# Another order for TensorE's steps around the two fills in the state-space layer of a two-layer kernel

## The chip, the cores and the metric

The kernel runs on one core of a Trainium2 chip. A core has five engines that run side by side, each through its own instructions in order: TensorE (PE, matrix products; PEld is its loading of weights), VectorE (DVE), ScalarE (ACT), GpSimd (POOL) and SyncE (SP, which issues DMA transfers here). They wait for each other by semaphores. The metric is the device time of one execution in microseconds (us). Everything is float32.

## The reference

The input x is 32 images of 96 channels by 56 x 56 places, L = 3136 places each. Layer 0 is an inverted-bottleneck convolution block (1x1 to 576 channels, 3x3 per channel, squeeze and excitation, 1x1 back, residual). Layer 1 treats the places as a sequence and applies two Mamba blocks, then a fusion with a pooled branch, a batch norm and a residual. The change lies in the Mamba blocks:

```
h   = layernorm(seq)                          # over the 96 channels
xs, z = split(h @ in_w)                       # 192 channels each
xc  = silu(causal_conv_4_taps(xs) + conv_b)
dt, Bm, Cm = split(xc @ xproj_w)              # 6, 16, 16 columns
delta = softplus(dt @ dt_w + dt_b)            # 192 channels
state[d, s] = exp(delta[d] * A[d, s]) * state[d, s] + delta[d] * xc[d] * Bm[s]   # along the places
y   = sum_s state[d, s] * Cm[s] + Dp * xc
seq = seq + (y * silu(z)) @ out_w
```

## The kernel before

Layer 0 takes the first sixth of the time and is the same in both kernels. Layer 1 cuts each image into NQ = 4 chunks of LC = 784 places, so there are 128 chunks, and each passes through two Mamba blocks: 256 **units** of work, `(chunk, block)` in the list `units`. From the fourth chunk on the blocks alternate, block 0 of chunk c and then block 1 of chunk c - 3, so units of the two kinds take turns.

The 192 channels times 16 states of a unit are scanned in NT = 24 **steps** of 128 partitions by 784 places. `place(t)` splits a step into k (0 to 2, a third of the channels), j (0 to 3, a group of four states) and p (0 or 1). One loop counter `at` runs through all 256 x 24 = 6144 steps, and each turn of the loop writes the instructions of one step to every engine:

- `decay` (ScalarE, L934): the factor exp(delta A), into a bank pair of PSUM (tag `da`, two buffers), one step ahead of its scan. For the steps with j = 0 it goes into SBUF instead, three or four steps ahead.
- `inject` (GpSimd, L971): u times B, where u = delta xc ("delta x"), for two steps at once, four steps ahead, for j = 1 to 3.
- `fill` (TensorE, L948): the same product for j = PEJ = 0, the first two steps of every eight. 64 small matmul instructions with a block-diagonal matrix of B (`diag`) and the transposed u (`ut`) write it into a `da` buffer, `bp`. So steps 0 and 1, 8 and 9, 16 and 17 of a unit read a fill, which is written by TensorE in the step before. `fill(at + 1)` needs the buffer that the scan of step at - 1 has read.
- `scan` (VectorE, L982), then `product` with C (VectorE, L990, first 400 places) and `rest` (GpSimd, L998, the other places).
- `reduce` (TensorE, L1019 for Dp xc and L1024 for the sum over states), four steps behind, at every odd step, and `gated` (VectorE, L1035) after each third of the channels.

Everything else of a unit is put among these steps by hand: `prepare(n)` and `finish(n)` return lists of `(t, step)`, where t counts steps from 48 before unit n's first scan (prepare) or from 24 after it (finish). The whole part of t picks the turn of the loop, the fraction sorts within it, and these steps come after `reduce` in that turn. Since everything repeats every 24 steps, one may think of t modulo 24: during the scans of one unit the kernel also projects and stores the unit before it, and prepares the two after it. `bursts` are ScalarE's runs of Silu and Softplus, each with two loads of a function table, before the scan of their turn.

The small steps on TensorE take their output banks from one pool of two (`pp`, by `bank(...)`): layer-norm statistics (`center`, `variance`, `turn`, `turn_back`: tiles cen, var, ct, xn), `conv` (xs), `gate` (z), `project_bc` (bc), `turn_b` (bt), `project_dt` (dt), `turn_u` (ut) and the output projection `project` in `finish` (o). Each bank is free again when ScalarE has copied it out (`square`, `normalise`, `normal`, `keep`, `store_bc`, `diagonal`, `keep_u`, `store`). TensorE works in order, so a step that waits for a bank holds all that is queued behind it, fills and reduces too.

`store` is two plain copies in a unit of block 0, and in a unit of block 1 it is two pairs of activations with accumulated sums, for the batch norm. `root` and `newton` are the inverse square root of the layer norm, on ScalarE and then VectorE. `input_u` makes u in thirds: before, two thirds on VectorE, which reads xc from a bank that ScalarE copies it to (`bring_x`, L802 and L810), and one third on GpSimd (L808). `spread` writes u to DRAM, from where it comes back (`ub`) in the layout of the scan.

Of the kernel before, what the change touches and what calls it, by code (L numbers as in the profile page):

```python
# [26 lines left out]
HB = LC // 2  # L27
# [6 lines left out]
NB = DIN // 64  # L34
# [25 lines left out]
def conv_mamba_kernel(ctx, tc, a, out):  # L60
# [43 lines left out]
    with ExitStack() as ph:  # L104
# [49 lines left out]
        xs, maps, h2s, pools, se = {}, {}, {}, {}, {}  # L154
# [303 lines left out]
    with ExitStack() as ph:  # L458
# [14 lines left out]
        def bank(name):  # L473
            return pp.tile([128, 512], F32, name=name, tag="p")
# [145 lines left out]
        def prepare(n):  # L620
# [14 lines left out]
            def center(h):  # L635
                ps = d["cen", h] = bank(f"cen_{n}_{h}")
                pe.matmul(ps[:C, :HB], cen, seqs[c, i][:, cols(h)], start=True, stop=True)

            def square(h):
                if h == 0:  # L640
                    d["sq"] = wt([128, LC], "sx", 1, n)[:C]
                s.activation(d["sq"][:, cols(h)], d["cen", h][:C, :HB], AF.Square)
# [17 lines left out]
            def newton(step):  # L660
                va, rs = d["va"], d["rs"]
                if step == 0:
                    d["nw"] = wt([TK, NK], "nw", 1, n)
                    v.scalar_tensor_tensor(d["nw"], rs, -0.5, va, ALU.mult, ALU.mult)
                if step == 1:
                    v.tensor_mul(d["nw"], d["nw"], rs)
                if step == 2:
                    to = wt([TK, NK], "rs", 1, n)
                    v.scalar_tensor_tensor(to, d["nw"], 1.5, rs, ALU.add, ALU.mult)
                    d["rs"] = to  # L670
                    if q == 0:
                        g.memset(xn[:, : KC - 1], 0.0)


            def turn(m):
                ps = d["ct", m] = bank(f"ct_{n}_{m}")
                for k in TURNS[m]:
                    o = (k - TURNS[m][0]) * C
                    pe.matmul(ps[:TK, o : o + C], seqs[c, i][:, k * TK : (k + 1) * TK], cen, start=True, stop=True)

            def normalise(m):
                if m == 0:
                    d["xt"] = wt([128, LC], "sx", 1, f"{n}_t")[:TK, : NK * C].rearrange("p (k c) -> p k c", k=NK)
                for k in TURNS[m]:
                    o = (k - TURNS[m][0]) * C
                    s.activation(d["xt"][:, k, :], d["ct", m][:TK, o : o + C], AF.Copy, scale=d["rs"][:, k : k + 1])

            def turn_back(h):
                ps = d["xn", h] = bank(f"xn_{n}_{h}")
                for k in range(NK):  # L690
                    lo, hi = max(k * TK, h * HB), min((k + 1) * TK, h * HB + HB)
                    if lo < hi:
                        pe.matmul(
                            ps[:C, lo - h * HB : hi - h * HB], d["xt"][:, k, :],
                            eye[:TK, lo - k * TK : hi - k * TK], start=True, stop=True,
                        )

            def normal(h):
                to = xn[:C, KC - 1 + h * HB : KC - 1 + h * HB + HB]
                s.copy(to, d["xn", h][:C, :HB])  # L700
# [50 lines left out]
            def spread(tag, t, ks):  # L751
                if tag not in d:
                    d[tag] = udram.tile([DIN, LC], F32, name=f"{tag}d_{n}", tag=f"{tag}d")
                for h in range(2):
                    to = d[tag][:, cols(h)].rearrange("(k m) l -> m k l", k=NB)
                    sp.dma_start(to[:, ks], t[h * 64 : h * 64 + 64, ks])
# [39 lines left out]
            def softplus():  # L796
                through([d["dl"]], AF.Softplus)

            def bring_x(k):

                d["up", k] = bank(f"up_{n}_{k}")
                s.copy(d["up", k][:, :HB], d["xc"][:, k])  # L802

            def input_u(k):

                if k == NB - 1:
                    d["us"] = wt([128, NB, HB], "us", 1, n)
                    g.tensor_mul(d["us"][:, k], d["dl"][:, k], d["xc"][:, k])  # L808
                    return
                v.tensor_mul(d["us"][:, k], d["dl"][:, k], d["up", k][:, :HB])  # L810
                spread("u", d["us"], slice(0, 1) if k == 0 else slice(1, NB))


            steps = [(-20, load)]
            for h in range(2):
                steps += [(-10.4 + h, lambda h=h: center(h)), (-9.8 + h, lambda h=h: square(h))]
            steps += [(-6.4, variance), (-5.8, root), *[(t, lambda m=m: newton(m)) for m, t in enumerate((-5.4, -5.3, -4.9))]]
            for m in range(2):
                steps += [(-4.5 + m, lambda m=m: turn(m)), (-3.9 + m, lambda m=m: normalise(m))]
                steps += [(-2.5 + m, lambda m=m: turn_back(m)), (-1.9 + m, lambda m=m: normal(m))]  # L820
            steps += [(-0.7, trail)]
            for k in range(NB):
                for taps, t in ((((0, 1), 1.5), ((2, 3), 2.5)), (((0,), 2.6), ((1,), 3.5), ((2, 3), 4.5)), (((0, 1), 9.5), ((2, 3), 10.5)))[k]:
                    steps += [(t, lambda k=k, taps=taps: conv(k, taps))]
                steps += [((3.1, 5.1, 11.1)[k], lambda k=k: keep("xc", 3, "xs", k))]
                steps += [((11.5, 12.5, 13.5)[k], lambda k=k: gate(k)), ((12.2, 13.1, 14.1)[k], lambda k=k: keep("z", 3, "zp", k))]
            steps += [(17.5, project_bc), (18.1, store_bc), (18.5, turn_b), (19.1, diagonal)]
            for k in range(NB):
                steps += [(19.6 + k, lambda k=k: project_dt(k)), (20.2 + k, lambda k=k: keep("dl", 1, "dtp", k))]
                steps += [((38.6, 46.6, 52.6)[k], lambda k=k: turn_u(k)), ((39.2, 47.2, 53.05)[k], lambda k=k: keep_u(k))]  # L830
            for m in range(6):
                steps += [(26.9 + m, lambda m=m: scatter(*divmod(m, 3)))]
            steps += [(32.1, lambda: spread("delta", d["dl"], slice(0, NB))), (33.0, lambda: input_u(NB - 1))]
            steps += [(33.6, lambda: bring_x(0)), (34.1, lambda: input_u(0))]
            steps += [(35.2, lambda: bring_x(1)), (36.1, lambda: input_u(1))]
            bursts = [(15, lambda: through([d["xc"], d["z"]], AF.Silu)), (31, softplus)]
            return steps, bursts

        def finish(n):

            c, i = units[n]
            b, q = divmod(c, NQ)
            d = data[n]

            def project(k):
                if k is None:
                    old = seqs.pop((c, i))
                    through = eye[:C, :C] if i + 1 < NL else fusw[:, 0, :]
                    for h in range(2):
                        d["o", h] = bank(f"o_{n}_{h}")  # L850
                        pe.matmul(d["o", h][:C, :HB], through, old[:, cols(h)], start=True, stop=False)  # L851
                    return
                for h in range(2):
                    r = slice(h * 64, h * 64 + 64)
                    pe.matmul(d["o", h][:C, :HB], outw[r, i, k, :], d["z"][r, k, :], start=False, stop=k == NB - 1)  # L855

            def store(h):
                if i + 1 < NL:
                    if h == 0:
                        seqs[c, i + 1] = wt([C, LC], f"seq{i + 1}", 4, n)  # L860
                    s.copy(seqs[c, i + 1][:, cols(h)], d["o", h][:C, :HB])
                    return
                if h == 0:
                    d["pre"] = wt([C, LC], "pre", 1, n)
                at = 2 * c + h
                s.activation(
                    d["pre"][:, cols(h)], d["o", h][:C, :HB], AF.Identity, bias=g2[:, b : b + 1],
                    accum_out=stats[:, 0, at : at + 1],
                )
                if at == 0:  # L870
                    s.activation(pivot, stats[:, 0, 0:1], AF.Copy, scale=-1.0 / HB)
                s.activation(d["o", h][:C, :HB], d["pre"][:, cols(h)], AF.Square, bias=pivot, accum_out=stats[:, 1, at : at + 1])  # L872

            def count():
                if i + 1 == NL:
                    sp.dma_start(pred[b][:, q * LC : (q + 1) * LC], d["pre"])
                data[n] = {}

            return [
                (5.5, lambda: [project(k) for k in (None, 0, 1)]), (6.5, lambda: project(2)),  # L880
                (7.1, lambda: store(0)), (8.1, lambda: store(1)), (9, count),
            ]

        LAG = 4
# [287 lines left out]
```

## Time and profile before

| | |
|---|---|
| median of 3 runs | 20446.33 us (20437.07 to 20451.98) |
| the profiled execution | 20447.55 us, span 20445.7 us |
| first scan to last scan, from the trace | 3462.3 to 20148.8 us |
| busy in the span: PE, DVE, ACT, POOL | 85%, 83%, 69%, 69% |
| mean granted clock of TensorE | 0.868 of full speed |
| DMA engines, mean busy share in layer 1 | 0.67 |

A row of the costliest groups reads: line, engine, operation, tile written <- tiles read, shape, count | busy us in all, mean ns of one | idle us of that engine just before them, and what ended most of it. A row of the timeline reads: start us, length us, engine, line, operation, tiles, shape, count, and in brackets the idle time of the engine before it and what ended that. A row of the windows reads: stretch, its length, then for PE, PEld, DVE, ACT and POOL the busy us with the number of instructions, then the granted clock of TensorE, the busy share of the DMA engines and GB/s.

### The profile page before, as it was taken

The numbers are of one execution on the slowest core, as the hardware profiler recorded it, in microseconds if no ns is written. First come the engines' busy times: TensorE is split into PE (matmuls) and PEld (weight loads), VectorE is DVE, ScalarE is ACT, GpSimd is POOL, SyncE is SP. The second block draws the span as 40 slices with busy tenths as digits, with TensorE's granted clock in tenths as the row PEclk, the third lists the DMA queues.
The fourth block names the chain that finished last, engine by engine and source line by source line (L and its number), as shares of the span: only waits on it lengthen the run. The fifth ranks groups of instructions, "written<-read, shape, count | busy, mean of one in ns | idle before, by whom it ended". The sixth has DMA issues, their size and how long they took to land. (4 is left out here: it accounts for less than half of the span.)

```text
span 20445.7 us, 515066 instructions
## 1 busy us (share of the span) xinstructions
PE 17445.1 (85%) x212796; PEld 8792.3 (43%) x212796; DVE 17046.5 (83%) x13151; ACT 14125.3 (69%) x26028; POOL 14171.2 (69%) x5870
## 2 busy tenths in 40 slices
PE   8999998888888888888888888888888888888883
PEld 4444444444444444444444444444444444444441
DVE  8888886888888888888888888888888888888883
ACT  4444444777777777777777777777777777777774
POOL 0000002888888888888888888888888888888884
PEclk9999998888888888888888888888888888888886
DMA  1000002666666666666666666666666666666668
GB/s 31 25 25 25 25 25 69 166 166 167 168 167 164 165 168 167 168 163 167 166 168 168 166 165 164 166 169 167 168 165 167 165 167 166 169 167 166 163 167 214
DMA packets 1607272, 2946.67 MB, mean 144 GB/s; under 512 B 688790, under 2 KB 901998, under 8 KB 1567814
## 3 DMA queue, kind: packets, MB, share of 16 engines
q1 hardware_dynamic: 1596278, 2875.12, 56.0%
q0 software_dynamic: 6656, 38.54, 0.9%
q8 instruction: 1668, 27.33, 0.6%
q14 instruction: 686, 5.62, 0.1%
q10 hardware_dynamic: 1984, 0.07, 0.0%
HBM read 2456.09 MB, written 455.82 MB: 142 GB/s over the span
## 5 line engine op out<-in xcount | busy, mean ns | idle before, releaser
L971 POOL TENSOR_TENSOR bx<-ub,B 128x1568 f32<-128x1568 f32 x2304 | 8152.6, 3538 | 20.0 <-DMA B<-bcd 20.0
L998 POOL TENSOR_TENSOR hc<-hh,C 128x768 f32<-128x768 f32 x3072 | 5612.6, 1827 | 2840.3 <-DVE hh L982 1831.3
L982 DVE TENSOR_TENSOR_SCAN hh<-da,state,bx 128x784 f32<-128x784 f32 x3456 | 6307.4, 1839 | 68.8 <-ACT da L934 67.2
L934 ACT ACTIVATE da<-deltab,acol 128x784 f32<-128x784 f32 x4608 | 4231.7, 918 | 2390.5 <-DVE hh L982 2376.6
L982 DVE TENSOR_TENSOR_SCAN hh<-bx,state,bp 128x784 f32<-128x784 f32 x1152 | 2124.7, 1844 | 1694.4 <-PE bp L948 1099.2
L990 DVE TENSOR_TENSOR hc<-hh,cp 128x800 f32<-128x800 f32 x3072 | 2954.6, 962 | 0.1
L1024 PE MATMUL y<-hc,rel 128*32 128x392 f32 x24576 | 2834.1, 529 | 27.3 <-issue 22.4
L948 PE MATMUL bp<-diag,ut 91*32 91x91 f32 (+1 forms) x98304 | 2574.4, 254 | 46.0 <-issue 31.1
L948 PEld LDWEIGHTS bp<-diag,ut 91*32 91x32 f32 (+1 forms) x98304 | 2333.3, 110 | 599.9 <-issue 507.5
L389 POOL TENSOR_TENSOR x<-x,x 96x784 f32<-96x784 f32 x128 | 274.5, 2144 | 3056.6 <-ACT x L388 3004.0
L712 PE MATMUL xs<-xn,wx 97*64 97x392 f32 x12288 | 2199.1, 499 | 0.9 <-ACT o L872 0.5
L314 DVE SCALAR_TENSOR_TENSOR h<-hpad,hp,h 128x1568 f32<-128x1568 f32 x1024 | 2037.0, 1989 | 34.3
L728 PE MATMUL z<-xn,wz 97*64 97x392 f32 x3072 | 973.1, 725 | 1268.2 <-DVE us L810 486.2
L982 DVE TENSOR_TENSOR_SCAN hh<-da,bx 128x784 f32<-128x784 f32 x1152 | 2032.0, 1778 | 25.5 <-ACT da L934 25.0
L959 ACT COPY cp<-C 128x400 f32<-128x400 f32 x3072 | 1505.7, 490 | 318.2 <-DVE hc L990 318.2
L934 ACT ACTIVATE bx<-deltab,acol 128x784 f32<-128x784 f32 x1536 | 1435.8, 935 | 0.0
L712 PEld LDWEIGHTS xs<-xn,wx 97*64 97x64 f32 x12288 | 814.0, 136 | 1350.5 <-issue 1256.3
L982 DVE TENSOR_TENSOR_SCAN hh<-bx,bp 128x784 f32<-128x784 f32 x384 | 684.6, 1783 | 626.7 <-PE bp L948 454.1
L288 PE MATMUL dw<-hpad,diag 32*32 32x392 f32 x36864 | 1097.3, 515 | 49.2 <-issue 48.5
L1024 PEld LDWEIGHTS y<-hc,rel 128*32 128x32 f32 x24576 | 605.1, 111 | 1064.7 <-issue 1023.3
L728 PEld LDWEIGHTS z<-xn,wz 97*64 97x64 f32 x3072 | 196.5, 176 | 1964.2 <-ACT xc L723 661.9
L749 PE MATMUL dt<-bcs,wd 64*64 64x392 f32 x3072 | 1020.5, 756 | 0.0
(194 smaller groups left out, 23019.2 us busy)
## 6 DMA issues: line engine op xcount, KB each, us to landing
deltab<-deltad SPq DMA_DIRECT2D x3072, 196.0 KB
ub<-ud SPq DMA_DIRECT2D x3072, 196.0 KB
C<-bcd SPq DMA_DIRECT2D x4096, 98.0 KB
diag<-bdiag SPq DMA_DIRECT2D x256, 1473.8 KB
B<-bcd SPq DMA_DIRECT2D x3072, 98.0 KB
deltad<-dl SPq DMA_DIRECT2D x512, 294.0 KB
ud<-us SPq DMA_DIRECT2D x512, 196.0 KB
ud<-us SPq DMA_DIRECT2D x512, 98.0 KB
```

Of the source, the lines that this page charges most:

```text
L288: pe.matmul(ps[r][to : to + 32, :HB], diag[src, n, t, :], hb[src, r0 : r0 + RB, dx : dx + W], start=t == 0, stop=t == 8, skip_group_check= ...
L314: v.scalar_tensor_tensor(acc, src, tap, acc, ALU.mult, ALU.add)
L712: pe.matmul(d["xs", k][h * 64 : h * 64 + 64, :HB], wx[:, i, o, k * 64 : k * 64 + 64], xn[:, o + h * HB : o + h * HB + HB], start=o == 0, s ...
L728: pe.matmul(ps[h * 64 : h * 64 + 64, :HB], wz[:, i, k * 64 : k * 64 + 64], xn[:, KC - 1 + h * HB : KC - 1 + h * HB + HB], start=True, stop ...
L934: s.activation(das[at], d["delta", k][:, p, :], AF.Exp, scale=acol[:, j, i, 2 * k + p : 2 * k + p + 1])
L948: pe.matmul(ps[sg * DB : sg * DB + DB, o : o + z], d["ut", k][:z, b, h, p * DB : p * DB + DB], dg[:z, sg // 2, h, x : x + z, sg % 2], star ...
L959: s.copy(cps[at], data[n]["C", j][:, :LP])
L971: g.tensor_mul(bx, data[n]["u", k], beside(data[n]["B", j]))
L982: v.tensor_tensor_scan(hhs[at - p][:, p, :], das.pop(at), bxs.pop(at), state[i][:, t : t + 1] if c % NQ else 0.0, ALU.mult, ALU.add,)
L990: v.tensor_mul(hcs[at - 1][:, :, :LP], hhs[at - 1][:, :, :LP], beside(cps.pop(at)))
L998: g.tensor_mul(hcs[at - 1][:, :, LP:], hhs[at - 1][:, :, LP:], beside(data[n]["C", j][:, LP:]))
L1024: pe.matmul(yps[k][r0 : r0 + DB, :HB], rel, hc[:, p, h * HB : h * HB + HB], start=False, stop=j == SG - 1, skip_group_check=True,)
```

## The change

The lists of `prepare` and `finish` get other times. By t modulo 24:

- The output projection (`project`) goes from steps 5 and 6 to 9 and 10, its `store` from 7 and 8 to step 11.
- The convolution of the third third of the channels goes from steps 9 and 10 to 4 and 5, right behind the second.
- `center`, `square`, `variance`, `root`, `newton`, `turn`, `normalise`, `turn_back`, `normal` and `trail` all come one to three steps earlier; `variance` from step 17 to 14, `root` and `newton` from 18 to 16.
- The second `gate` comes right behind the first, in step 11, the third in step 12.
- `turn_u` goes from steps 14, 22 and 4 to 13, 14 and 5. Steps 6 and 22 now have no small TensorE step, nor have 7, 8, 15, 16, 23 and 0, the turns in which the fills themselves are written.
- All three thirds of u are made by GpSimd, in steps 9, 10 and 11, each followed by its own two writes to DRAM. `bring_x` and its bank are gone.

```diff
-            def bring_x(k):
-
-                d["up", k] = bank(f"up_{n}_{k}")
-                s.copy(d["up", k][:, :HB], d["xc"][:, k])
-
             def input_u(k):
 
-                if k == NB - 1:
+                if k == 0:
                     d["us"] = wt([128, NB, HB], "us", 1, n)
-                    g.tensor_mul(d["us"][:, k], d["dl"][:, k], d["xc"][:, k])
-                    return
-                v.tensor_mul(d["us"][:, k], d["dl"][:, k], d["up", k][:, :HB])
-                spread("u", d["us"], slice(0, 1) if k == 0 else slice(1, NB))
-
+                g.tensor_mul(d["us"][:, k], d["dl"][:, k], d["xc"][:, k])
+                spread("u", d["us"], slice(k, k + 1))
 
             steps = [(-20, load)]
             for h in range(2):
-                steps += [(-10.4 + h, lambda h=h: center(h)), (-9.8 + h, lambda h=h: square(h))]
-            steps += [(-6.4, variance), (-5.8, root), *[(t, lambda m=m: newton(m)) for m, t in enumerate((-5.4, -5.3, -4.9))]]
+                steps += [((-11.4, -10.5)[h], lambda h=h: center(h)), ((-10.8, -9.9)[h], lambda h=h: square(h))]
+            steps += [(-9.4, variance), (-7.9, root), *[(t, lambda m=m: newton(m)) for m, t in enumerate((-7.5, -7.4, -7.3))]]
             for m in range(2):
-                steps += [(-4.5 + m, lambda m=m: turn(m)), (-3.9 + m, lambda m=m: normalise(m))]
-                steps += [(-2.5 + m, lambda m=m: turn_back(m)), (-1.9 + m, lambda m=m: normal(m))]
-            steps += [(-0.7, trail)]
+                steps += [(-6.5 + m, lambda m=m: turn(m)), (-5.9 + m, lambda m=m: normalise(m))]
+                steps += [(-4.5 + m, lambda m=m: turn_back(m)), (-3.9 + m, lambda m=m: normal(m))]
+            steps += [(-2.7, trail)]
+            taps = (
+                (((0, 1), 1.5), ((2, 3), 2.5)), (((0,), 2.6), ((1, 2), 3.5), ((3,), 4.5)), (((0, 1), 4.6), ((2, 3), 5.5)),
+            )
             for k in range(NB):
-                for taps, t in ((((0, 1), 1.5), ((2, 3), 2.5)), (((0,), 2.6), ((1,), 3.5), ((2, 3), 4.5)), (((0, 1), 9.5), ((2, 3), 10.5)))[k]:
-                    steps += [(t, lambda k=k, taps=taps: conv(k, taps))]
-                steps += [((3.1, 5.1, 11.1)[k], lambda k=k: keep("xc", 3, "xs", k))]
-                steps += [((11.5, 12.5, 13.5)[k], lambda k=k: gate(k)), ((12.2, 13.1, 14.1)[k], lambda k=k: keep("z", 3, "zp", k))]
-            steps += [(17.5, project_bc), (18.1, store_bc), (18.5, turn_b), (19.1, diagonal)]
+                steps += [(t, lambda k=k, o=o: conv(k, o)) for o, t in taps[k]]
+                steps += [((3.1, 5.1, 6.1)[k], lambda k=k: keep("xc", 3, "xs", k))]
+                steps += [((11.5, 11.6, 12.5)[k], lambda k=k: gate(k)), ((12.1, 12.2, 13.1)[k], lambda k=k: keep("z", 3, "zp", k))]
+            steps += [(17.6, project_bc), (18.2, store_bc), (18.6, turn_b), (19.2, diagonal)]
             for k in range(NB):
                 steps += [(19.6 + k, lambda k=k: project_dt(k)), (20.2 + k, lambda k=k: keep("dl", 1, "dtp", k))]
-                steps += [((38.6, 46.6, 52.6)[k], lambda k=k: turn_u(k)), ((39.2, 47.2, 53.05)[k], lambda k=k: keep_u(k))]
+                steps += [((37.6, 38.7, 53.6)[k], lambda k=k: turn_u(k)), ((38.2, 40.2, 54.2)[k], lambda k=k: keep_u(k))]
             ...
-            steps += [(32.1, lambda: spread("delta", d["dl"], slice(0, NB))), (33.0, lambda: input_u(NB - 1))]
-            steps += [(33.6, lambda: bring_x(0)), (34.1, lambda: input_u(0))]
-            steps += [(35.2, lambda: bring_x(1)), (36.1, lambda: input_u(1))]
+            steps += [(32.1, lambda: spread("delta", d["dl"], slice(0, NB)))]
+            steps += [(33.0 + k, lambda k=k: input_u(k)) for k in range(NB)]
...
             return [
-                (5.5, lambda: [project(k) for k in (None, 0, 1)]), (6.5, lambda: project(2)),
-                (7.1, lambda: store(0)), (8.1, lambda: store(1)), (9, count),
+                (9.5, lambda: [project(k) for k in (None, 0, 1)]), (10.5, lambda: project(2)),
+                (11.1, lambda: store(0)), (11.2, lambda: store(1)), (12, count),
             ]
```

## The prediction

> **What bounds the kernel now.** I read the page first: the span by engine, the clock row and the costliest groups.
>
> ```profile
> PE 17445.1 (85%) x212796; PEld 8792.3 (43%) x212796; DVE 17046.5 (83%) x13151; ACT 14125.3 (69%) x26028; POOL 14171.2 (69%) x5870
> PEclk9999998888888888888888888888888888888886
> L982 DVE TENSOR_TENSOR_SCAN hh<-bx,state,bp 128x784 f32<-128x784 f32 x1152 | 2124.7, 1844 | 1694.4 <-PE bp L948 1099.2
> L982 DVE TENSOR_TENSOR_SCAN hh<-bx,bp 128x784 f32<-128x784 f32 x384 | 684.6, 1783 | 626.7 <-PE bp L948 454.1
> ```
>
> No engine is full, but nearly all of VectorE's idle time in layer 1 stands before the scans that read a fill (bp): 1694.4 + 626.7 = 2321 us, 9.07 us in each of the 256 units. With the scans counted off in order, 24 to a unit (means over units 10 to 239), a unit lasts 65.27 us: 55.44 us without VectorE idle, and idle of 3.29 us before scan 8, 2.87 before scan 16, 2.87 before scan 0 and 0.77 around step 18 (newton waiting for root). The second scan of each pair waits for almost nothing. So the question is why the first fill of a pair is late. The timeline of one unit, TensorE and then VectorE, shows it:
>
> ```profile
> 10062.75 0.87 PE L1024 MATMUL y<-hc,rel 128*32 128x392 f32 x8
> 10066.11 2.23 PE L851 MATMUL o<-seq,fusw 96*96 96x392 f32 x4 [2.49 <-ACT ut L794]
> 10068.26 3.19 PE L855 MATMUL o<-z,outw 64*96 64x392 f32 x12
> 10071.39 1.70 PE L948 MATMUL bp<-diag,ut 120*32 120x120 f32 x64
> ...
> 10081.23 0.88 PE L728 MATMUL z<-xn,wz 97*64 97x392 f32 x4 [1.74 <-ACT xc L723]
> 10084.56 1.57 PE L728 MATMUL z<-xn,wz 97*64 97x392 f32 x4 [2.45 <-ACT z L723]
> 10086.06 1.57 PE L1019 MATMUL y<-xc,dd 64*64 64x392 f32 x4
> ...
> 10090.53 2.93 PE L637 MATMUL cen<-seq,cen 96*96 96x392 f32 x4
> 10093.25 1.05 PE L787 MATMUL ut<-eye,us 128*120 128x128 f32 x4
> 10094.23 1.68 PE L948 MATMUL bp<-diag,ut 120*32 120x120 f32 x64
> ```
>
> ```profile
> 10068.24 1.78 DVE L982 TENSOR_TENSOR_SCAN hh<-da,bx 128x784 f32<-128x784 f32 x1
> 10073.21 1.79 DVE L982 TENSOR_TENSOR_SCAN hh<-bx,bp 128x784 f32<-128x784 f32 x1 [3.19 <-PE bp L948]
> ```
>
> Scan 6's buffer is free at 10067.4, but TensorE is in the output projection (o) until 10071.4, and scan 8 waits 3.19 us for the fill queued behind it. TensorE itself had stood idle for 2.49 us for a bank. The same matmuls also run at two speeds: z takes 0.88 us and then 1.57. The windows view gives the clock of the last stretches:
>
> ```profile
> 10083.10:10086.50 3.40, 1.95 (x6) 0.58 (x8) 3.40 (x4) 3.40 (x6) 2.67 (x2) 0.62 0.00 0
> 10086.50:10092.00 5.50, 5.50 (x19) 1.23 (x16) 5.28 (x4) 2.09 (x5) 4.32 (x2) 0.50 0.75 189
> ```
>
> The clock halves where TensorE was little busy and comes back after a stretch without a gap. Cut into the clock record's own grid of 3.41 us, windows under about 48% busy were followed by half clock, those over 50% were not, except windows filled by var and bt (matmuls of 1 and 8 columns). A unit has three half spells: steps 6 to 7, 12 to 14, 19.5 to 22. So: a wait for a bank, half clock, all later work twice as long, late fill. I call steps 0 to 7 segment A, 8 to 15 B, 16 to 23 C; each ends in a stall.
>
> **Prices**, full and half clock, from the timeline: z, dt or dd x4 0.88 and 1.57; reduce 0.87 and 1.53; cen x4 1.56 and 2.93; o 3.8 in all (1.56 + 2.22) and about 7.2; a fill 1.68 and 2.85 (only at the very ends of the layer); ut 0.65 and 1.05. Small ones: xs 0.18 an instruction, var 1.54, bt 0.84, xn 0.97. ScalarE: decay 0.87 from start to start, copies 0.48, Silu burst 4.9, store of a block-1 unit 2.64.
>
> **Delta x on GpSimd.** VectorE loses two multiplies of 0.56 us (L810): -1.1 us a unit, in B. ScalarE loses two copies of 0.49 that had slack. GpSimd gains two of 1.02 us (L808's row): its busy time goes from 54.1 us a unit (13,850 us in the stretch from the first scan to the last, by the windows view) to 56.2, and no unit can be shorter than that. SP writes u in six transfers for four; the last waits for GpSimd's third multiply, which by the walk below comes some 3 us later than VectorE's did, since GpSimd's products and injections stand between. Behind it on SP stand the store of pred, and the next delta and u loads, needed six steps on: nothing waits yet. The large diag load is issued after the second fill of C and landed about 10 us later, judged by when SP could go on behind it; the walk leaves it 13.9, so there is some 3.5 us of cover.
>
> **Segment A.** Projection out (-3.8), third convolution in (+2.86), and nothing behind turn_u in step 5. Walk from scan 0 at 0, steps at VectorE's own pace: fill and reduce to 2.45, the three convolutions with their reduces to 13.35, turn_u after the copy of xc at 13.7, done 14.35. Scan 6 ends at 15.3 and frees the buffer: fill 15.4 to 17.05, scan 8 due 17.85. Nothing is late; the 1.4 us of idle leave every window over 55% busy. I take -3.2.
>
> **Segment C.** Here the variance leaves (-1.54), as does the first turn_u. Walk from scan 16: second fill to 2.3, ct after newton at 3.5, bc to 6.7, second ct after normalise 7.25, bt to 8.9, then xn and dt one behind the other through ScalarE's copies, last dt 15.95, fill at 16.2 when scan 22 frees its buffer; scan 0 is due 18.7. No stall at full clock. But 6.7 to 10.1 holds 0.75 us idle, 0.8 of ct and 0.84 of bt: about half a window of work, as in the var windows that always dropped. At half clock the chain ends 3 to 4 us later, a stall like today's. Between 0 and 2.87 I take the middle, 1.5, since the window lies at the limit: -1.4.
>
> **Segment B** is where it is paid back. It takes the projection (+3.8), the variance (+1.54) and a second turn_u (+0.65), and gives up the third convolution (-2.86): fill 1.68, o 3.8, three reduces 2.6, gates 2.64, dd 0.88, cen 1.56, variance 1.54 and two turn_u 1.3 are 16.0 us at full clock, and scan 14 frees the buffer at 15.2. It is also a chain through two banks: the first gate waits until store has emptied o. Walk from scan 8: projection to 6.1, reduce to 6.95. ScalarE reaches store at 7.6 (behind decay 12 and cp). Where the unit behind is one of block 0, store is two copies: gates at 8.1 and 9.0, third gate behind z's copy at 11.0, cen 11.9, dd and reduce to 14.3, second cen to 15.1, turn_u 15.7, variance behind its square 15.9 to 17.4, turn_u to 18.0, fill to 19.65: scan 16 due at 17.75 starts 1.95 late. Where it is one of block 1, store holds ScalarE 2.64 us: gates at 9.0 and 10.3, third 12.45. Any window there is under half busy, so the clock halves from about 10 to 17 us: third gate to 14.0, cen 15.45, dd and reduce to 17.9, second cen 18.7, variance to 20.8, fill to 23.1. That is 5.4 late (decays 14 and 15, which now stand behind store, cost VectorE 0.8 of it already). Units of the two kinds alternate: mean 3.7. The windows around the variance are again near half busy; a third of what a drop there costs (both fills at 2.85 and a reduce at 1.53) adds 0.9. So 2.87 becomes 4.6: +1.7. Newton, now behind the Silu burst (root done 2.8 us after a late scan 16), waits 0.3 where it waited 0.77: -0.5.
>
> **Sum.** -3.2 - 1.4 + 1.7 - 0.5 - 1.1 = -4.5 us a unit, 60.8 for 65.27; times 256 is -1152 us. The profiled execution took 20447.55 us (span 20445.7), 1 us from the median of 20446.33, so about 19,300.
>
> **Rivals.**
> 1. The clock holds (chance 0.20). A and C without a stall, B late by 1.95 and, at full clock, 3.35: mean 2.65, newton 0.3. Idle is 3.0 for 9.8, so with the 1.1 a unit saves 7.9: 57.4 us, just over GpSimd's 56.2, 18,430 in all. For it: my longest single gap is 2.05 us, shorter than today's 2.49. Against: windows count, not gaps, and 1.74 with 2.45 already dropped it. The Trainium skill, "TensorE: Matmul & The Clock Gate", Part 1, says the clock falls after at least one idle window of about 3.4 us, and its closing table warns only of gaps above about 3 us. By that rule this rival is what happens; the trace disagrees, since the clock fell around gaps of 2.49 us.
> 2. Slower (0.17). One mechanism: half clock through all of B, into its two fills. B's chain with every matmul at its half-clock price ends with a fill from 22.4 to 25.25 in the plain units and 1.2 later in the others, so scan 16 is 8.1 late on the mean, and scan 17 waits 1.3 more for its fill. C keeps its 2.87, A and newton have 0.4: idle of 12.7 against 9.8 + 1.1 today, +1.8 us a unit, 20,910. It decides once the waits for the two fills behind B pass 2.87 + 3.2 + 0.5 + 1.1 = 7.7 us while C stays as it is. For it: B becomes the fullest segment and has three bank waits in a row; against: both neighbours are emptier, and a full-speed window resets the clock.
> 3. A is not cured (0.12): a drop before fill 8 makes both fills 2.85 and the projection behind them slow; 2.2 to 3.3 us are lost again, about 20,050.
> 4. What A gains, B takes whole: 20,440 (0.03).
>
> My forecast has 0.48, its own range 18,900 to 19,900. Two in ten may fall outside; most of rival 1 and all of 3 and 4 belong inside, so 18,350 to 20,450. Faster by over 0.2% (41 us, about what this measurement tells from none): 0.48 + 0.20 + 0.12 = 0.80; within 0.03; slower 0.17.
>
> **What would show it.** Right: scan 8 without a wait, half spells gone from steps 6 to 7, the longest wait before scan 16, larger where store is the block-1 one; L808 three times a unit at 1.02 us; GpSimd above 90% busy. Wrong: scan 8 still waiting (A), z at 0.88 throughout (rival 1), fills of 2.85 us in the middle of the layer (rival 2), VectorE waiting for GpSimd's bx or for a DMA, which my sum has at nothing.

## The result, and the profile after

| | before | after |
|---|---|---|
| median of 4 runs, us | 20449.15 (20437.07 to 20475.1) | 18985.22 (18978.54 to 19002.94) |
| profiled span, us | 20445.7 | 18976.7 |
| mean granted clock of TensorE | 0.868 | 0.93 |
| one unit, us (mean over units 10 to 239) | 65.27 | 59.51 |

The ratio is 0.9284, 95% interval 0.9268 to 0.9300: faster by 1464 us, where 1146 had been forecast (19,300 from 20,446). Of the unit, 5.76 us are gone, and 256 times that is 1475. These lines of the page answer to those shown of before:

```profile
PE 16483.9 (87%) x212796; PEld 8321.5 (44%) x212796; DVE 16782.1 (88%) x12639; ACT 13781.1 (73%) x25516; POOL 14628.1 (77%) x6382
PEclk9999999899999999999999999999999999999996
L975 DVE TENSOR_TENSOR_SCAN hh<-bx,state,bp 128x784 f32<-128x784 f32 x1152 | 2118.4, 1839 | 838.1 <-PE bp L941 821.5
L975 DVE TENSOR_TENSOR_SCAN hh<-bx,bp 128x784 f32<-128x784 f32 x384 | 681.9, 1776 | 329.2 <-PE bp L941 323.9
```

(The fill is L941 now, the scan L975; the lines behind the removed `bring_x` have moved up by seven.) The idle time before scans that read a fill has halved, from 2321 us to 1167, while the scans take what they took. Counting the scans off in order gives VectorE's idle by place. This table holds the experiments too; all figures are us a unit, and "other" is all idle time of VectorE that does not stand before scans 0, 8 and 16:

| kernel | unit | VectorE busy | scan 8 | scan 16 | scan 0 | other |
|---|---|---|---|---|---|---|
| before | 65.27 | 55.38 | 3.29 | 2.87 | 2.87 | 0.86 |
| after | 59.51 | 54.35 | 0.01 | 4.33 | 0.20 | 0.62 |
| e1_delta_only | 63.37 | 54.33 | 3.83 | 2.13 | 2.76 | 0.32 |
| e2_delta_back | 62.72 | 55.39 | 0.05 | 1.88 | 0.00 | 5.39 |
| e3_stats_only | 66.51 | 55.44 | 3.02 | 5.88 | 0.41 | 1.76 |
| e4_stats_back | 61.23 | 54.40 | 0.02 | 2.71 | 2.32 | 1.78 |
| e5_hold | 58.81 | 54.39 | 0.01 | 3.33 | 0.53 | 0.56 |
| e6_turn_u_back | 59.72 | 54.44 | 0.01 | 3.74 | 0.36 | 1.17 |
| e7_step6_load | 59.87 | 54.44 | 0.87 | 3.92 | 0.04 | 0.60 |
| e9_vector_direct | 66.74 | 61.31 | 0.00 | 5.08 | 0.00 | 0.35 |
| e10_late_square | 58.35 | 54.29 | 0.01 | 3.19 | 0.56 | 0.30 |
| e11_late_hold | 58.40 | 54.36 | 0.00 | 2.16 | 1.32 | 0.56 |
| e12_late_hold_lp424 | 57.78 | 54.92 | 0.02 | 1.88 | 0.53 | 0.42 |

The timeline of after shows how. First comes TensorE in segments A and B of a plain unit (one where the unit behind is of block 0):

```profile
9411.46 0.65 PE L787 MATMUL ut<-eye,us 128*120 128x128 f32 x4 [0.27 <-ACT xc L723]
9413.01 1.68 PE L941 MATMUL bp<-diag,ut 120*32 120x120 f32 x64 [0.90 <-DVE hh L975]
...
9417.86 1.56 PE L844 MATMUL o<-seq,eye 96*96 96x392 f32 x4
9419.35 2.22 PE L848 MATMUL o<-z,outw 64*96 64x392 f32 x12
9421.50 0.86 PE L1017 MATMUL y<-hc,rel 128*32 128x392 f32 x8
9423.43 1.54 PE L728 MATMUL z<-xn,wz 97*64 97x392 f32 x8 [1.07 <-ACT seq L854]
9426.29 1.57 PE L728 MATMUL z<-xn,wz 97*64 97x392 f32 x4 [1.32 <-ACT z L723]
9427.80 1.62 PE L637 MATMUL cen<-seq,cen 96*96 96x392 f32 x2
9429.35 1.57 PE L1012 MATMUL y<-xc,dd 64*64 64x392 f32 x4
...
9434.14 1.54 PE L647 MATMUL var<-mean,sx 96*112 96x1 f32 x14
...
9436.10 1.66 PE L941 MATMUL bp<-diag,ut 120*32 120x120 f32 x64
```

The fill for scan 8 starts as soon as scan 6 has freed its buffer (released by DVE hh, not by a bank), and TensorE has waited 0.90 us for it, so there is slack. In B, TensorE waits twice for ScalarE's copies, and behind the second wait the matmuls run at half-clock prices until the full clock is back ahead of the variance: z at 1.57, dd at 1.57. VectorE's timeline has the two ends, scan 8 without a wait and scan 16 with the longest of the unit:

```profile
9415.45 1.76 DVE L975 TENSOR_TENSOR_SCAN hh<-bx,bp 128x784 f32<-128x784 f32 x1
```

```profile
9437.88 1.79 DVE L975 TENSOR_TENSOR_SCAN hh<-bx,bp 128x784 f32<-128x784 f32 x1 [4.83 <-PE bp L941]
```

The windows view of after (the last three figures of a row are the clock, the DMA share and GB/s), first in B, then in C of the same unit:

```profile
9421.40:9426.00 4.60, 2.50 (x18) 0.64 (x16) 4.60 (x5) 4.18 (x8) 4.60 (x4) 1.00 0.47 136
9427.20:9430.60 3.40, 3.40 (x10) 0.69 (x6) 3.40 (x3) 3.15 (x7) 3.40 (x3) 0.50 0.05 12
9434.00:9438.00 4.00, 3.86 (x90) 3.53 (x94) 0.12 (x1) 3.97 (x7) 4.00 (x2) 1.00 0.92 237
```

```profile
9442.00:9445.40 3.40, 2.99 (x21) 1.46 (x20) 3.40 (x3) 3.07 (x10) 2.90 (x3) 1.00 1.08 236
9445.40:9448.80 3.40, 3.21 (x32) 2.07 (x31) 3.39 (x4) 3.28 (x10) 3.40 (x2) 1.00 1.03 222
9448.80:9452.20 3.40, 3.40 (x27) 1.43 (x24) 3.40 (x4) 2.99 (x9) 1.40 (x1) 1.00 0.76 201
```

In B the clock falls behind the stretch with the two waits (2.50 us of work in 4.60) and is back for the fills. In C of this unit it does not fall. Of the three half spells a unit one is left, in steps 12 to 15 (steps 13 and 14 are at half clock in 73 to 83% of the units); in steps 16 to 22 some 2% of the units at most are at half clock, and some 10% in step 23. Where the unit behind is of block 1, the first gates wait for `store`'s activations instead:

```profile
9482.71 0.88 PE L728 MATMUL z<-xn,wz 97*64 97x392 f32 x4 [2.01 <-ACT o L865]
9484.02 1.40 PE L728 MATMUL z<-xn,wz 97*64 97x392 f32 x4 [0.43 <-ACT o L865]
9486.06 1.57 PE L728 MATMUL z<-xn,wz 97*64 97x392 f32 x4 [0.65 <-ACT z L723]
```

Scan 16 waits 3.34 us on the mean in plain units and 5.32 in the others, where scan 15 waits another 0.52 for its decay behind `store`.

### The profile page after: what moved, and what is told of

Its sections match the earlier page's. It is cut to its first block, busy times and chain, and to the rows that moved or that the text cites. A ratio compares the mean times of both kernels' runs of the same rounds, so it can differ in the third digit from the quotient of the medians.

```text
span 18976.7 us, 514307 instructions
## 1 busy us (share of the span) xinstructions
PE 16483.9 (87%) x212796; PEld 8321.5 (44%) x212796; DVE 16782.1 (88%) x12639; ACT 13781.1 (73%) x25516; POOL 14628.1 (77%) x6382
## 4 chain that ended last, share of the span: by engine, by line
issue 36%; DVE 25%; ACT 15%; PE 12%; DMA 7%; SPq 2%; POOL 2%; ACTq 0%; POOLq 0%; DVEq 0%
DVE hh L975 13%; DVE hc L983 8%; DMA diag<-bdiag 3%; PE cen L637 3%; DVE h L314 2%; ACT da L927 2%; DMA ub<-ud 2%; PE y L1017 2%; PE z L728 2%; PE y L1012 2%; ACT L612 2%; PE bp L941 1%; SPq L896 1%; ACT L613 1%; ACT cp L952 1%
## 5 line engine op out<-in xcount | busy, mean ns | idle before, releaser
L975 DVE TENSOR_TENSOR_SCAN hh<-da,state,bx 128x784 f32<-128x784 f32 x3456 | 6319.7, 1841 | 50.1 <-ACT da L927 48.6
L941 PE MATMUL bp<-diag,ut 91*32 91x91 f32 (+1 forms) x98304 | 2634.3, 258 | 681.1 <-DVE hh L975 568.5
L941 PEld LDWEIGHTS bp<-diag,ut 91*32 91x32 f32 (+1 forms) x98304 | 2335.5, 111 | 1407.1 <-DVE hh L975 1136.6
L975 DVE TENSOR_TENSOR_SCAN hh<-bx,state,bp 128x784 f32<-128x784 f32 x1152 | 2118.4, 1839 | 838.1 <-PE bp L941 821.5
L975 DVE TENSOR_TENSOR_SCAN hh<-da,bx 128x784 f32<-128x784 f32 x1152 | 2035.1, 1778 | 25.3 <-ACT da L927 25.1
L728 PE MATMUL z<-xn,wz 97*64 97x392 f32 x3072 | 869.1, 670 | 694.7 <-ACT o L865 283.3
L386 PE MATMUL c<-h,w3s 128*96 128x392 f32 (+1 forms) x2560 | 964.3, 522 | 39.5 <-DVE w3s L371 39.5
L975 DVE TENSOR_TENSOR_SCAN hh<-bx,bp 128x784 f32<-128x784 f32 x384 | 681.9, 1776 | 329.2 <-PE bp L941 323.9
L235 PE MATMUL c<-x,w 96*128 96x392 f32 x2048 | 812.8, 553 | 102.1 <-ACT hpad L237 79.8
## 6 DMA issues: line engine op xcount, KB each, us to landing
diag<-bdiag SPq DMA_DIRECT2D x256, 1473.8 KB
```

The costliest lines, as they stand in the source:

```text
L728: pe.matmul(ps[h * 64 : h * 64 + 64, :HB], wz[:, i, k * 64 : k * 64 + 64], xn[:, KC - 1 + h * HB : KC - 1 + h * HB + HB], start=True, stop ...
L941: pe.matmul(ps[sg * DB : sg * DB + DB, o : o + z], d["ut", k][:z, b, h, p * DB : p * DB + DB], dg[:z, sg // 2, h, x : x + z, sg % 2], star ...
L975: v.tensor_tensor_scan(hhs[at - p][:, p, :], das.pop(at), bxs.pop(at), state[i][:, t : t + 1] if c % NQ else 0.0, ALU.mult, ALU.add,)
```

## Experiments

### The parts of the change

**Delta x alone.** The kernel before, with u made by GpSimd as in the change and nothing else.

```diff
-            steps += [(33.6, lambda: bring_x(0)), (34.1, lambda: input_u(0))]
-            steps += [(35.2, lambda: bring_x(1)), (36.1, lambda: input_u(1))]
+            steps += [(33.0 + k, lambda k=k: input_u(k)) for k in range(NB)]
```

> The kernel before with one part of the change: all three thirds of u on GpSimd in steps 9, 10 and 11, no copies of xc into a bank. My theory counts the two multiplies of 0.56 us on VectorE as time of the unit, -1.1 us or a little more, since two users of the two banks go as well: about 20,160 us or lower. Rival: segment B ends in a wait for a fill, so VectorE's 1.1 us only fall into that wait: 20,450 us. Segments A and C should keep their waits of 3.29 and 2.87 us in either case.

Measured 19964.17 us, ratio 0.9764 (0.9748 to 0.9780): 1.9 us a unit. VectorE's busy time fell by 1.05, as priced; its idle by another 0.85. The second goes with the two banks of `bring_x`, which no longer stand in TensorE's way: before, TensorE waited 476 us ahead of the gates for VectorE to make u, and here that wait is gone, though cen now waits for z's copies.

```profile
PE z L728 <- DVE us L810: 475.8, 127, 4.0
```

(A wait of TensorE in before: us in all, times, longest.) Scan 8 got 0.54 worse and scan 16 0.74 better. So VectorE's saving is not hidden in the waits, and it comes with some more.

**Statistics alone, and the change without them.** The lines from `center` to `trail`, put at the new times in the kernel before (e3), and at the old times in the kernel after (e4).

```diff
-            steps += [(-6.4, variance), (-5.8, root), ...]
+            steps += [(-9.4, variance), (-7.9, root), ...]
...
-            steps += [(-0.7, trail)]
+            steps += [(-2.7, trail)]
```

> The kernel before with only the layer-norm statistics moved earlier as in the change (center to trail). My theory: segment C loses its wait (-2.7 us a unit) and most of newton's (-0.5), segment B takes the variance (1.54 us) in front of its fill and waits some 1.5 us longer, A keeps 3.29: -1.7 us a unit, about 20,010 us. Rival: what cured C is the empty step 22, and with turn_u still in step 22 the clock falls in C as before: 20,450 us or more.

Measured 20762.08, ratio 1.0152 (1.0137 to 1.0167): 1.5% slower. Scan 0 went from 2.87 to 0.41 (0.20 in after), although the second `turn_u` still stood in step 22; but scan 16 went from 2.87 to 5.88, twice the growth I had expected, and `gated` began to wait for its reduce (L1024):

```profile
DVE hh L982 <- PE bp L948: 2118.4, 543, 17.0
DVE z L1035 <- PE y L1024: 289.5, 254, 3.0
```

(The waits of VectorE in e3: us in all, times, longest.)

> The changed kernel with the layer-norm statistics at their times of before (variance in step 17, root in 18, turn_back in 21 and 22). My theory: A stays cured, C has its wait of 2.9 us and newton 0.8 us again, B loses the variance in front of the fill (-1.5 us or more): +1.7 us a unit against the changed kernel, about 19,420 us. Rival: the statistics cost as much in B as they save in C, so the time stays within 60 us of 18,985.

Measured 19440.67, ratio 0.9507 (0.9492 to 0.9522), 20 us from the figure expected. Scan 8 waits for nothing, while e1 and e3 leave its wait in place, so A's cure lies in the other moves; my walk puts it down to the projection and the convolutions, which were not tried by themselves. Scan 0 waits 2.32 again, newton and scans around it 1.66, and scan 16 only 2.71: the earlier statistics take from C and newton what they partly give back in B.

Put one on the other the parts are: delta x -485 us, then the other moves -523 (e1 to e4), then the statistics -455 (e4 to after). Alone, the statistics cost 312. They were seen to pay with delta x and the other moves in place, which take the banks of `bring_x` and the third convolution out of B; which of these they need was not taken apart.

**Delta x back on VectorE** in the kernel after, with the bank copies in step 8 and the multiplies in 9 and 10.

```diff
+            steps += [(32.6, lambda: bring_x(0)), (32.7, lambda: bring_x(1))]
+            steps += [(33.1, lambda: input_u(0)), (34.1, lambda: input_u(1))]
```

> The changed kernel with two thirds of u back on VectorE (multiplies in steps 9 and 10, the copies of xc into banks in step 8, ahead of the projection). By my sum it gives back 1.1 us a unit: about 19,270 us. Rival: the multiplies go into VectorE's wait before scan 16, which is 4.3 us here, and the time stays at 18,985 us.

Measured 19814.05, ratio 0.9688 (0.9673 to 0.9702): 3.2 us a unit worse than after, far more than VectorE's 1.1. A new wait of 4.78 us a unit stands before scan 12; TensorE's timeline and VectorE's answer:

```profile
9744.78 1.62 PE L853 MATMUL o<-seq,eye 96*96 96x392 f32 x2 [2.35 <-DVE us L810]
9747.92 1.59 PE L853 MATMUL o<-seq,eye 96*96 96x392 f32 x2 [1.52 <-ACT cp L961]
...
9752.60 0.86 PE L1026 MATMUL y<-hc,rel 128*32 128x392 f32 x8
```

```profile
9753.53 0.56 DVE L1037 TENSOR_TENSOR z<-z,y 128x392 f32<-128x392 f32 x1 [4.06 <-PE y L1026]
```

The projection cannot have its banks until VectorE has read xc from them, and the reduce that `gated` needs is queued behind it. So this run does not price the multiplies by themselves: the new place of the projection needs delta x off the banks.

**Delta x on VectorE without the banks**, both inputs from SBUF.

```diff
-                g.tensor_mul(d["us"][:, k], d["dl"][:, k], d["xc"][:, k])
+                (g if k == NB - 1 else v).tensor_mul(d["us"][:, k], d["dl"][:, k], d["xc"][:, k])
```

> The changed kernel with the first two thirds of u multiplied by VectorE straight from SBUF, no banks, in steps 9 and 10. My term for delta x: VectorE's two multiplies are time of the unit, 1.1 us at 0.56 each, more if two SBUF inputs make them or GpSimd's operations longer: 19,270 us or above. Rival: they go into the wait of 4.3 us before scan 16, and the time stays at 18,985 us.

Measured 20847.0, ratio 1.0191 (1.0176 to 1.0206), 1.9% slower than before. A line of the costliest groups and then the timelines of GpSimd and VectorE:

```profile
L803 DVE TENSOR_TENSOR us<-dl,xc 128x392 f32<-128x392 f32 x512 | 1819.3, 3553 | 21.2 <-ACT dl L612 21.2
```

```profile
10177.49 3.50 POOL L964 TENSOR_TENSOR bx<-ub,B 128x1568 f32<-128x1568 f32 x1
```

```profile
10178.58 2.84 DVE L803 TENSOR_TENSOR us<-dl,xc 128x392 f32<-128x392 f32 x1
10181.35 1.78 DVE L975 TENSOR_TENSOR_SCAN hh<-da,bx 128x784 f32<-128x784 f32 x1
```

The multiply takes 3.55 us on the mean where it took 0.56 with one input from a bank, and here it ends 0.43 us after GpSimd's injection: it waits the injection out. The mean hides two cases. Of the 512 multiplies, 135 meet no instruction of GpSimd and take 0.55 us; 375 meet an injection and end some 0.42 us after one, and 138 of these are held through an injection, a product and the next injection, 7.85 us on the mean. VectorE's busy time rises by 7.0 us a unit. The Trainium skill, "SBUF — State Buffer", section "Who interferes with whom", says that a VectorE instruction with two SBUF inputs contends with a GpSimd instruction that reads SBUF, and that what they contend for is locked and not shared out; the trace agrees. So taking u off the banks meant taking it off VectorE.

### The clock in B

**A filled wait.** The kernel after, with four matmul instructions more in step 11, ahead of the first gate, on a part of the y bank that nothing reads.

```diff
+            def hold(m):
+                if 0 in yps:
+                    for _ in range(m):
+                        pe.matmul(yps[0][:, HB:512], eye, eye[:, : 512 - HB], start=True, stop=True, skip_group_check=True)
+            steps += [(11.45, lambda: hold(4))]
```

> The changed kernel with four extra matmuls (128 by 120, results never read) in step 11 between the reduce and the first gate, about 1 us of TensorE inside its wait of 1.07 us (units with a block-0 unit behind) or 2.01 us (block-1). Theory (the clock): B's wait is long because the clock halves behind that wait; with it filled no window there is under half busy, gates, dd and reduce run at full clock, and scan 16 waits about 2.0 us for 3.45 in the plain units and 3.4 for 6.0 in the others: -2.0 us a unit, about 18,460 us, granted clock up from 0.93. Rival (banks and ScalarE alone set B): 18,985 us or up to 100 us more.

Measured 18811.23, ratio 0.9196 (0.9180 to 0.9212): 174 us better than after, with more work on TensorE. TensorE's timeline of the same plain unit:

```profile
9396.03 1.15 PE L810 MATMUL y<-eye 128*128 128x120 f32 x8
9397.18 1.54 PE L728 MATMUL z<-xn,wz 97*64 97x392 f32 x8
9400.03 0.88 PE L728 MATMUL z<-xn,wz 97*64 97x392 f32 x4 [1.32 <-ACT z L723]
9400.84 0.90 PE L637 MATMUL cen<-seq,cen 96*96 96x392 f32 x2
9401.67 0.88 PE L1019 MATMUL y<-xc,dd 64*64 64x392 f32 x4
```

The wait of 1.07 us is filled, the one of 1.32 us is still there, and the clock holds: z and dd are 0.88 instead of 1.57. Over the plain units, 29% are at half clock in step 14 where 70% were in after, and scan 16 waits 2.02 for 3.34. That is the clock's price in B, shown by adding nothing but work. In the other units 85% are still at half clock there (98% in after), so the extra matmuls did not hold it; scan 16 went only from 5.32 to 4.63 (decay 15 from 0.52 to 0.30), and their scan 0 rose from 0.39 to 0.99: (1.3 + 0.9) / 2 - 0.3 is some 0.8 us a unit, 0.70 by the table, where 2 were expected.

**The store's squares later.** In block-1 units the two Square activations of `store` go to step 23, writing over `pre` in SBUF instead of into the bank of o.

```diff
+            def square_sum(h):
+                at = 2 * c + h
+                s.activation(kept["pre"][:, cols(h)], kept["pre"][:, cols(h)], AF.Square, ...)
...
+            last = [(23.8 + h / 10, lambda h=h: square_sum(h)) for h in range(2)] if i + 1 == NL else []
```

> The changed kernel with store of the block-1 units shortened in step 11: the two activations that square and sum go to the end of step 23, in place over the tile that has been written out, so the banks of o are free after two activations (1.3 us of ScalarE for 2.64). Theory: the block-1 units wait 6.0 us in B against 3.45 in the others because the gates wait for store; with a short store they come to about 3.5, -1.25 us a unit on the mean, about 18,670 us; the 1.2 us at the end of the unit lie in ScalarE's idle time behind step 23. Rival (the difference comes from elsewhere, or ScalarE has no room in step 23): 18,985 us or more.

Measured 18724.03, ratio 0.9158 (0.9144 to 0.9172). The two kinds of unit are now alike, scan 16 waiting 3.39 and 2.99 us, and the wait of scan 15 is gone. So the extra lateness of block-1 units was the length of `store`, for whose last use of the banks the gates waited (L865 above). How much of it was the banks, and how much the decays queued behind `store` on ScalarE, this run doesn't tell.

**Both together** (e11), **and both with 24 places more of each product on VectorE** (e12: `LP = 424` for 400).

> As e10_late_square, with the four extra matmuls of e5_hold in front of the first gate. Theory (clock and store are the two causes of B's length): every unit is like the plain ones of e5_hold, which waited 2.15 us and took 57.6 us: about 18,490 us. Rival (GpSimd, with 56 us of work a unit, is the next bound and its lag eats it): no better than e10_late_square by more than 60 us.

Measured 18715.76, ratio 0.9154 (0.9140 to 0.9167): no different from e10, so the 18,490 that was expected was missed. Scan 16 fell from 3.19 to 2.16 as expected, but scan 0 rose from 0.56 to 1.32. TensorE's waits over layer 1, first of after and then of this kernel, and a fill for scan 0 in its timeline:

```profile
PE bp L941 <- DMA diag<-bdiag: 85.7, 43, 3.2
```

```profile
PE bp L955 <- DMA diag<-bdiag: 480.0, 181, 6.2
```

```profile
9402.50 2.85 PE L955 MATMUL bp<-diag,ut 120*32 120x120 f32 x64 [4.17 <-DMA diag<-bdiag]
```

The next stall is the load of `diag` (1473.8 KB). It has one buffer, so SP can issue it only after the second fill behind scan 16 is done, and it stands behind other loads in SP's queue. Here the fill that needs it began 12.2 us after its issue at 9390.30. A unit that is shorter leaves it less time, and the wait of over 4 us also drops the clock under the fill (2.85 us).

> As e11_late_hold, with the first 424 places of each product on VectorE for 400: GpSimd has about 1.4 us less a unit (its product takes 1.83 us for 768 elements), VectorE about 0.7 more (0.96 us for 800). If GpSimd binds in e11_late_hold, this is faster by up to 0.7 us a unit, 180 us. If VectorE and the chain through B bind, it is slower by 0.7 us a unit, 180 us.

Measured 18571.73, ratio 0.9089 (0.9074 to 0.9104): the shortest of all, 2.2% under after. GpSimd is busy 54.72 us a unit for 55.93, VectorE 54.92 for 54.36; scan 0's wait is down to 0.53, and TensorE's waits for diag to 317 us. So with B's stalls made smaller GpSimd's load does count. Whether it counts by its own time, or by making u late and with it what SP queues behind u, this run doesn't tell.

### The empty step and the cover in A

> The changed kernel with only the second turn_u and its copy back at steps 22 and 23, so step 22 is not empty. Theory (what counts is that the chain is done when scan 22 frees the buffer): TensorE stands idle 0.72 us there and turn_u takes 0.65, so scan 0 waits at most 0.2 us more, and B loses 0.65 us in front of its fill: -0.5 us a unit, about 18,850 us. Rival (the last step must be empty): scan 0 waits 0.7 us or more again, by a later fill or a half clock, and the time is 18,985 us or above.

The kernel after with the second `turn_u` in its old step.

```diff
-                steps += [((37.6, 38.7, 53.6)[k], ...), ((38.2, 40.2, 54.2)[k], ...)]
+                steps += [((37.6, 46.6, 53.6)[k], ...), ((38.2, 47.2, 54.2)[k], ...)]
```

Measured 19041.73, ratio 0.9308 (0.9293 to 0.9324), against 0.9268 to 0.9300 for after: no better, and hardly to be told from it, where 18,850 was expected. Scan 0 waits 0.36, so step 22 need not be empty. B gained 0.59, but newton and others lost 0.55, and a half spell came back in steps 19.5 to 20.5, in up to 72% of the units.

> The changed kernel with twelve of the same extra matmuls (about 3 us of TensorE) in step 6, behind the first turn_u and ahead of fill 8. Theory (A was cured by being done in time, with 0.9 us idle and 0.8 us between the end of the fill and its scan): scan 8 waits 3.0 less 1.7, about 1.3 us, and as the scans behind it move along the unit grows by as much: +330 us, about 19,320 us. Rival (the gain in A came from the full clock, not from the empty step): the fill keeps up and the time stays at 18,985 us.

The kernel after with twelve matmul instructions in step 6 (`hold(12)` at 6.5). Measured 19089.86, ratio 0.9332 (0.9318 to 0.9346), +105 us where +330 was expected. Scan 8 waits 0.87 for 0.01, so A's slack is real and used up by less than these; B gave half of it back (scan 16 at 3.92 for 4.33).

## Why the prediction was right, and where it was off

Per unit, from the table (B with scan 15's decay wait, newton out of "other"):

| term | forecast | measured |
|---|---|---|
| segment A, scan 8 | -3.2 | -3.28 |
| segment C, scan 0 | -1.4 | -2.67 |
| segment B, scan 16 and decay 15 | +1.7 | +1.72 |
| newton | -0.5 | -0.56 |
| VectorE's multiplies | -1.1 | -1.03 |
| sum | -4.5 | -5.82, and 0.06 of other idle |

**The step that was mis-sized is segment C:** -1.4 forecast, -2.67 measured. I put a stall between 0 and 2.87 and took the middle, because one window of C lay near half busy, and said that at half clock the chain would end 3 to 4 us later. Both halves were too dark. The clock did not drop: the windows of C above are 88 to 100% busy, though ct and bt (0.83 and 0.79 us), which I had taken for as good as idle there, are part of that work. And where it does drop there, it costs less: in e6 a short half spell stands in C and scan 0 waits 0.36. The long one of e4, in steps 20 to 22 in some 75% of the units, goes with 2.32, but there the statistics are late as well. What cured C is the earlier statistics, shown from both sides: with them scan 0 waits at most 0.56 in all kernels without filled waits in B (e3 among these, where all else is as before), without them 2.3 to 2.9.

**Segment A** is right in size, and in its reason as far as the runs go (the moves were made together): with the projection out, scan 8 waits 0.01; e1 and e3, where it stays, have 3.83 and 3.02. "Nothing is late" had a slack that e7 bounds.

**Segment B** is right in sum by luck, by two errors of opposite sign. My walk gave the plain units full clock and 1.95 us; most of them drop, at the two gate waits of 1.07 and 1.32 us in the unit shown, and they wait 3.34 on the mean. For the others it gave 5.4 at half clock, against 5.32 and 0.52 for the decay. The 0.9 I added (a third of 2 x 1.17 + 0.66 is 1.0, in fact) was for a drop at the variance, and there it does not fall: var, at 9434.14 in the unit shown, stands in the row of the windows that is at full clock again. e5 shows the drop at the gates and what it is worth in a plain unit (1.3 us), e10 that `store` makes the difference of the two kinds.

**VectorE and newton** are right in size; e1 gives the multiplies by themselves, with 0.85 us of stalls on top that I had not counted, because I looked for what the bank copies cost ScalarE and not for TensorE's gates waiting behind them. e2 and e9 show that neither old way of making u would have gone with the new order.

**Cover.** GpSimd's three multiplies of 1.02 us are there (tile us), and over layer 1 it is busy 14255 of 15285 us, 93% (55.92 us a unit, 56.2 forecast):

```profile
L803 POOL TENSOR_TENSOR us<-dl,xc x768: 999/1017/1081, 3435.9 to 18595.6; 128x392 f32<-128x392 f32 x192
```

Almost no wait for bx came of it (1.1 us in all). My 3.5 us of cover for the diag load was too much: after waits for it 43 times, 85.7 us in all, and every version with a shorter unit waits more.

**Rivals.** Rival 1 had the clock hold everywhere. It holds in A and C and not in B: there it fell behind waits of 1.07 and 1.32 us, and in the unit shown, filling the first alone held it (e5). The Trainium skill, "TensorE: Matmul & The Clock Gate", Part 1, "What's actually happening", has the clock fall after at least one idle window of about 3.4 us. By that rule it should have held in B too, since no wait for a bank there is over 2.9 us; the trace differs. My own rule, half clock behind windows under 48% busy and none over 50% but for var and bt, does not carry over as it stands: in layer 1 of after, 70 of the 253 full-clock windows of 3.41 us that half clock followed were over 50% busy, up to 61%. None of these 70 spent a fifth of its time in var and bt, and 471 windows that did so kept the clock. So in these traces a busy share near a half marks where drops begin, and does not decide each window. Rival 2 needed fills at half clock and C as it was: all but some 3% of the fills in the layer run at full clock, and C is cured. Rival 3 fell with scan 8, rival 4 with the sum. e3 shows a loss of rival 2's kind in B (+3.0) when only the statistics move: there the first fill for scan 16 took over 2.4 us in 123 of 230 units.

**Open.** The 523 us from e1 to e4 are projection, convolution, gates and `turn_u` together; they weren't taken apart, so what each of them is worth, and the projection's share in A's cure, is not shown. Nor was a version tried that issues the diag load earlier.

## What to carry to other kernels

Where one engine's queue holds steps from several pieces of work, read each stall to the step queued ahead of it and to the bank that this one waits for; a place is good or bad by who frees the bank last, and parts of such a reordering do not add up (the statistics cost 312 us alone and saved 455 behind the others). Count TensorE's busy share by windows: in B two short waits close together cost more than their length, and filling one with idle work was worth it. When a stall goes, look up the next transfer or engine whose cover was the stall's own time.

## What the runs showed of the hardware that was not expected

- Four extra matmuls (eight records, 1.15 us) in a wait of 1.07 us kept z and dd at 0.88 us instead of 1.57 in the unit shown.
- A float32 multiply of 128 x 392 on VectorE with both inputs in SBUF took 0.55 us with GpSimd idle, 1.2 to 8.4 us where it met a GpSimd injection of 3.55 us (3.55 on the mean of all 512), and 0.56 with one input in PSUM.
- A load of 1.47 MB, among others in one queue, was waited for until 12 us after its issue, and in the shortened unit it became the next wait.
